# A convolution's products by patches of 4 rows x 2 columns in a four-image convolution, attention and filter kernel

## The chip, the cores and the metric

One Trainium2 chip (trn2), one core. The metric is device time in microseconds. Engines: PE (TensorE matmul), PEld (its weight loads), DVE (VectorE), ACT (ScalarE), POOL (GpSimd), SP (SyncE, which here only issues DMAs). Each engine works through its own queue in order, and waits on semaphores for the others.

## The reference, cut to what matters

Four images of 256 channels, 48 x 48. Layer 0: group norm, 3x3 convolution, scale and shift, ReLU, q, k and v, attention with 8 heads, projection, added to the input. Layer 1: group norm, a 3x3 convolution that gives five sets of nine softmax weights per pixel, five dilated filters with these weights, a 1x1 convolution of the six results, batch norm over all images, added.

```
x = lax.conv_general_dilated(Vx, conv_w, window_strides=(1, 1), padding='SAME', ...)
x = x + conv_b[None, :, None, None]
...
x = jax.nn.relu(x)
...
attn = softmax(einsum('bhdn,bhdm->bhnm', q, k) * scale)
...
guidance = _conv(x, W_cat, pad=1)
for i, d in enumerate((1, 6, 12, 24, 36)):
    w = softmax(guidance[:, 9 * i:9 * (i + 1)], axis=1)
    outs.append(_dyn_branch(x, w, d))
y = _conv(concatenate(outs), W_scale, pad=0)
```

The change touches how the first convolution, `conv_general_dilated`, is computed for images 1 to 3.

## The kernel before

All is float32. Channels lie on 128 partitions in two halves (`NH` = 2). An image passes three stages: the convolution with q, k and v (`conv_qkv`), attention (`attention`), the filters (`dynamic_filters`). Image 0's convolution runs alone. After it, attention of image b alternates with a stage in which the filters of image b run together with the convolution and qkv of image b + 1; the last filters run with two chunks left over from image 2.

The convolution (`conv`) makes four output rows at a time from six input rows. Along rows it uses six sums of input rows, `v[0]` to `v[5]`, each from rows `d[0]` to `d[5]` of the padded, normalized image (`pads[b % 2]`), made in stages by `inputs`: on DVE for image 0, on POOL for the others, with ACT for the multiples by 2 and 4. `ORDER` = (1, 2, 3, 4, 0, 5) is the order of the products. For each of the six there are three weight columns `u[i]`, so a product over 3 columns and two channel halves is six matmuls of 128 x 128 by 288 columns, for each half `g` of the rows and each half `o` of the outputs. `outputs` empties PSUM and combines the six products into four rows; two PSUM banks (tag `c`) take turns. The weights `u` are made once, in image 0 (`Made`), stored in `u_d`, and loaded again by `taken(i)` on SP, 768 KB each, into two buffers.

All code runs through one recording order: each engine's queue follows the order of the Python calls. In the filter stage `drive` decides it. It holds a clock per engine in estimated nanoseconds (`Clock`), and five streams (`loads`, `far`, `near`, `filters`, `mixes`), each of which yields the time from which its next step is due. If none is due by PE's clock, the next step of the filler `other` (convolution, then qkv, of the next image) is issued; a step of it is one or a few matmuls. Before `drive`, at the seam, `run(ns)` issues filler unconditionally: 2400 ns, then 600 and 700 around the parts of `norm.finish`, then 2500 after the normalization.

The seam is this: the last unit of attention is closed (`close`: sums on PE, transposes and reciprocal on DVE), its last chunk is projected (`project`, PE), added to the image and put through `bn_stats` on DVE; `norm.finish` aggregates on DVE, averages over groups on PE, squares on ACT (L665), a second matmul, a square root on ACT (L98), a reciprocal on DVE; then DVE (L636) and ACT (L1661) normalize a half of the image each, and the first matmuls of the filters (`pg`, L1197) can read it. POOL clears `lg`, `bmat` and `amat` (L1179).

In the filter stage, for each of six chunks: `weights` makes softmax weights (`pg`, `pt`, `pw`, `lg`), `far` builds matrices by predicated copies on DVE and multiplies on PE (L1395), copies on ACT or DVE (`moved`, L1170, L1172), `near` multiplies on DVE nine taps (L1461, one operand from PSUM) which POOL adds (L1466), `mixes` does the 1x1 convolution (`py`, L1561). ACT copies each tap's weights into PSUM (`wb`, L1448), one bank of them.

In attention, POOL also issues accumulating DMAs (L1052, L1054) that take over a part of the softmax sums from DVE (L1050).

Of the kernel before, what the change touches and what calls it, by code (L numbers as in the profile page):

```python
# [16 lines left out]
N = HH * WW  # L17
P = 128
# [39 lines left out]
def conv_preact_kernel(  # L58
# [483 lines left out]
    u_d = tc.dram_tile([6, P, NH, 3, C], F32, name="u_d")  # L542
# [3 lines left out]
    with tc.tile_pool(name="w", bufs=1) as wpool, tc.tile_pool(  # L546
        name="act", bufs=1
    ) as act, tc.tile_pool(name="u", bufs=2) as upool, tc.manual_schedule():
# [12 lines left out]
        wqkv = wpool.tile([P, NH, 3, C], F32, tag="wqkv", name="wqkv")  # L561
        wp = wpool.tile([P, NH, C], F32, tag="wp", name="wp")
# [53 lines left out]
        bn_s6 = wpool.tile([P, NH], F32, tag="bn_s6", name="bn_s6")  # L616


        pads = []
        for j in range(2):  # L620
            t = act.tile([P, NH, PADW * PADW], F32, tag=f"pad{j}", name=f"pad{j}")
            t = t.rearrange("p h (r w) -> p h r w", w=PADW)
            nc.gpsimd.memset(t[:, :, 0, :], 0.0)
            nc.gpsimd.memset(t[:, :, PADW - 1, :], 0.0)
            nc.gpsimd.memset(t[:, :, 1 : PADW - 1, 0], 0.0)
            nc.gpsimd.memset(t[:, :, 1 : PADW - 1, PADW - 1], 0.0)
            pads.append(t)

# [58 lines left out]
        class Clock:  # L687
# [11 lines left out]
            def level(self):  # L699
                self.t = dict.fromkeys(self.t, max(self.t.values()))  # L700
# [21 lines left out]
        def taken(i):  # L722

            u = upool.tile([P, NH, 3, C], F32, tag="u", name=f"u_{i}")
            nc.sync.dma_start(out=u, in_=u_d[i])
            return u

        class Made:


            def __init__(self, wc, pool):
                self.w = [wc[:, :, 3 * j : 3 * j + 3, :] for j in range(3)]
                self.u = {}
                self.pool = pool

# [9 lines left out]

            def home(self, i):
                return upool.tile([P, NH, 3, C], F32, tag="u", name=f"u_{i}")
# [4 lines left out]
            def __call__(self, i):  # L752
                w, u = self.w, self.u
                if i in (2, 4):
                    nc.vector.tensor_tensor(u[i], u[i], w[1], ALU.subtract)
                if i == 2:
                    nc.scalar.mul(w[0], w[0], 0.25)
                    nc.scalar.mul(w[1], w[1], 0.5)
                if i in (0, 5):
                    u[i] = self.home(i)  # L760
                    nc.scalar.mul(u[i], w[i and 2], -6.0)
                nc.sync.dma_start(out=u_d[i], in_=u[i])
                return u[i]
# [148 lines left out]

        def conv_qkv(b, gn, psum_tile, weights, ready, pool, between=()):

            hid = keep("h", f"hid_{b}")
            yield from conv(b, gn, psum_tile, weights, ready, pool, hid, between)
# [6 lines left out]
            for c in range(NCK):  # L923
                cols = slice(c * CH, (c + 1) * CH)
                for g in range(NH):
                    for s, dst, bias in ((0, q, Q_B), (1, k_, K_B)):
# [18 lines left out]
                        )  # L945
                        yield 2 * MM
# [31 lines left out]
        def attention(b, q, k_, vT, pools, spare, project, scratch):  # L978
# [132 lines left out]
            weigh(*steps[-1], prev)  # L1111
            close(last)
            return ao, chunk
# [25 lines left out]
        def dynamic_filters(b, ao, chunk, norm, other, pools):  # L1139
# [485 lines left out]
            def drive(streams):  # L1625

                due = [next(s, None) for s in streams]
                while any(d is not None for d in due):
                    soonest = NEVER
                    for j, d in enumerate(due):  # L1630
                        if d is None:
                            continue
                        d = d() if callable(d) else d
                        if d <= clock.t["PE"]:
                            due[j] = next(streams[j], None)
                            break
                        soonest = min(soonest, d)
                    else:
                        got = next(other, None)
                        if got is not None:  # L1640
                            spent[0] += got
                        elif soonest < NEVER:
                            clock.t["PE"] = soonest

            if alone:
                other = late()


            while chunk < NCK:
# [142 lines left out]
        u_next = None  # L1792
        norms = {}
        for b in range(B + 1):

            with tc.tile_pool(name=f"work1_{b}", bufs=2) as work1, tc.tile_pool(
# [13 lines left out]
                if b < B:  # L1810
                    weights, between = taken, ()
                    if b == 0:
# [62 lines left out]
                if b == 0:  # L1875
                    for j, _ in enumerate(other):
                        if j == 0:
# [5 lines left out]
                            nc.vector.tensor_scalar(bn_s6, bn_s, -1.0 / 6.0, None, ALU.mult)  # L1883
                            table(AF.Exp)
# [8 lines left out]
                else:  # L1893
                    if b == B:
# [15 lines left out]
                        for j in range(2):  # L1910
                            t = upool.tile([P, NH, 3, C], F32, tag="u", name=f"yu_{j}")
                            t = t.rearrange("p h k c -> p (h k c)")
                            homes += [unit(t[:, : NH * CH]), unit(t[:, NH * CH :])]
# [48 lines left out]
            scratch = upool.tile([P, NH, 3, C], F32, tag="u", name=f"scratch_{b}")  # L1962
            scratch = scratch.rearrange("p h k c -> p (h k c)")
            spare = []
            if b + 1 < B:
                load_pad(b + 1)
                u_next = taken(ORDER[0])
# [13 lines left out]
            with tc.tile_pool(name=f"work0_{b}", bufs=2) as work0, tc.tile_pool(  # L1981
# [4 lines left out]
                    lambda c, ao, pp, b=b, n=norm1: project(b, c, ao, pp, n), scratch,  # L1986
# [76 lines left out]
```

## Time and profile before

| | |
|---|---|
| median of 3 runs | 2771.2 us (2770.79 to 2772.4) |
| the profiled execution's own time | 2766.55 us |
| its span | 2764.8 us |
| granted TensorE clock, mean | 0.99 |
| HBM read and written | 107.40 MB, 34.46 MB |
| image 0's convolution and qkv | 0 to 148 us |
| attention 0 | 148 to 515 us |
| filters 0 with convolution 1, to its last `py` | to 747 us |
| rest of convolution 1, and its qkv | to 817 us |

The stages of images 1 and 2 follow in the same manner, and the last filters with the batch norm end the kernel. A line of the page's list of groups, or of a timeline, gives: start and length (timeline), engine, source line, operation, written tile <- read tiles, partitions x elements, count, and in brackets the engine's idle time before it with what ended it. One float32 matmul of the program appears as two records of PE. A clock of 0.5 in a window is half rate.

### The profile page before, as it was taken

The numbers are of one execution on the slowest core, as the hardware profiler recorded it, in microseconds if no ns is written. First come the engines' busy times: TensorE is split into PE (matmuls) and PEld (weight loads), VectorE is DVE, ScalarE is ACT, GpSimd is POOL, SyncE is SP. The second block draws the span as 40 slices with busy tenths as digits, with TensorE's granted clock in tenths as the row PEclk, the third lists the DMA queues.
The fourth block names the chain that finished last, engine by engine and source line by source line (L and its number), as shares of the span: only waits on it lengthen the run. The fifth ranks groups of instructions, "written<-read, shape, count | busy, mean of one in ns | idle before, by whom it ended". The sixth has DMA issues, their size and how long they took to land. (4 is left out here: it accounts for less than half of the span.)

```text
span 2764.8 us, 42248 instructions
## 1 busy us (share of the span) xinstructions
PE 2638.8 (95%) x17108; PEld 1135.8 (41%) x17108; DVE 2025.3 (73%) x1956; ACT 1761.1 (64%) x2153; POOL 632.3 (23%) x583
## 2 busy tenths in 40 slices
PE   7999999899999999989999999999999999999994
PEld 5632223455662222345565222245566222234452
DVE  6578888656539888856644988894664988885476
ACT  3488988633349888843336889882335988873244
POOL 5100100435400100054430001006542001000352
PEclk9999999999999999999999999999999999999997
DMA  5604544223422444423360345442335244432465
GB/s 216 156 24 103 109 98 104 58 77 90 104 56 58 101 102 97 109 57 75 84 132 9 81 98 112 101 87 56 93 92 150 55 96 95 101 87 68 118 181 182
DMA packets 132522, 267.35 MB, mean 97 GB/s; under 512 B 55656, under 2 KB 97552, under 8 KB 131424
## 3 DMA queue, kind: packets, MB, share of 16 engines
q0 software_dynamic: 25952, 135.74, 21.6%
q1 hardware_dynamic: 106368, 128.84, 17.7%
q8 instruction: 136, 2.23, 0.3%
q14 instruction: 66, 0.54, 0.1%
HBM read 107.40 MB, written 34.46 MB: 51 GB/s over the span
## 5 line engine op out<-in xcount | busy, mean ns | idle before, releaser
L1050 DVE TENSOR_TENSOR acc<-acc,p 128x2048 f32<-128x2048 f32 (+1 forms) x572 | 1061.1, 1855 | 115.6 <-ACT p L1014 64.9
L1014 ACT ACTIVATE p<-se 128x1536 f32<-128x1536 f32 x648 | 938.7, 1449 | 0.1
L1005 PE MATMUL so<-q,k 32*128 32x512 f32 (+1 forms) x1440 | 726.4, 592 | 13.5 <-ACT p L1013 12.7
L1005 PE MATMUL se<-q,k 32*128 32x512 f32 (+1 forms) x4320 | 735.1, 592 | 0.0
L1034 PE MATMUL num<-p,vT 128*32 128x512 f32 (+1 forms) x5760 | 705.1, 560 | 4.6 <-ACT p L1014 2.4
L1013 ACT ACTIVATE p<-so 128x512 f32<-128x512 f32 x648 | 388.4, 599 | 186.8 <-PE se L1005 80.0
L1466 POOL TENSOR_TENSOR near<-near,prod 128x768 f32<-128x768 f32 x192 | 348.8, 1817 | 431.4 <-DVE prod L1461 424.7
L1005 PEld LDWEIGHTS so<-q,k 32*128 32x128 f32 x1440 | 216.1, 183 | 529.0 <-ACT p L1013 489.8
L1034 PEld LDWEIGHTS num<-p,vT 128*32 128x32 f32 x5760 | 133.8, 108 | 478.8 <-issue 444.3
L1054 POOL DMA_DIRECT2D scratch<-p x124 | 105.5, 851 | 772.3 <-ACT p L1014 519.8
L1461 DVE TENSOR_TENSOR prod<-wb,pad 128x768 f32<-128x768 f32 x192 | 181.9, 953 | 87.6 <-ACT wb L1448 75.6
L1561 PE MATMUL py<-far,wsc 128*128 128x384 f32 x704 | 236.7, 488 | 0.0
L1005 PEld LDWEIGHTS se<-q,k 32*128 32x128 f32 x4320 | 226.7, 183 | 5.4 <-ACT p L1014 4.1
L1448 ACT COPY wb<-ws 128x384 f32<-128x384 f32 x216 | 108.7, 507 | 171.3 <-DVE prod L1461 137.6
L1170 ACT COPY far<-far 128x512 f32<-128x512 f32 x82 | 87.9, 1099 | 137.4 <-PE far L1395 134.6
L1052 POOL DMA_DIRECT2D scratch<-p x32 | 17.9, 559 | 669.7 <-ACT p L1014 508.3
L1561 PEld LDWEIGHTS py<-far,wsc 128*128 128x128 f32 x704 | 131.1, 190 | 87.3 <-issue 1.8
L897 PE MATMUL pc<-cv_q,u 128*128 128x288 f32 x576 | 151.8, 415 | 8.2 <-DVE cv_q L788 6.2
L1197 PE MATMUL pg<-pad,wcat 128*45 128x384 f32 x864 | 149.1, 493 | 10.0 <-ACT lg L1255 4.4
L897 PE MATMUL pc<-cv_k,u 128*128 128x288 f32 x576 | 153.3, 410 | 4.3 <-DVE yt L832 2.7
L930 PE MATMUL pq<-hid,wqkv 128*128 128x384 f32 x384 | 125.6, 487 | 1.7 <-DVE yt L832 0.6
L897 PEld LDWEIGHTS pc<-cv_q,u 128*128 128x128 f32 x576 | 108.7, 192 | 43.2 <-DVE cv_q L788 6.3
(252 smaller groups left out, 2368.3 us busy)
## 6 DMA issues: line engine op xcount, KB each, us to landing
scratch<-p POOLq DMA_DIRECT2D x156, 768.0 KB, 5.7
ws<-w_d SPq DMA_DIRECT2D x216, 192.0 KB
pad<-in_x SPq DMA_DIRECT2D x14, 1152.0 KB
u<-u_d SPq DMA_DIRECT2D x18, 768.0 KB
xst<-in_x POOLq DMA_DIRECT2D x36, 192.0 KB, 6.9
x_d<-pad SPq DMA_DIRECT2D x36, 192.0 KB
y_d<-y SPq DMA_DIRECT2D x14, 384.0 KB
u_d<-u SPq DMA_DIRECT2D x6, 768.0 KB
```

What stands on the lines that cost most here:

```text
L897: nc.tensor.matmul(m, u[:, h, kx, o * P : (o + 1) * P], halves[g][:, h, i, :, kx : kx + WW], start=(h == 0 and kx == 0), stop=(h == NH - 1 ...
L930: nc.tensor.matmul(pq[:, :CH], wqkv[:, i, s, g * P : (g + 1) * P], hid[:, i, cols], start=(i == 0), stop=(i == NH - 1),)
L1005: nc.tensor.matmul(dst[:, at : at + n], k_[r, g, m * P : (m + 1) * P], q[r, g, q0 : q0 + n], start=True, stop=True,)
L1013: nc.scalar.activation(p[:, 0, :], s1, AF.Exp, scale=QS)
L1014: nc.scalar.activation(p[:, 1:, :], s3, AF.Exp, scale=QS)
L1034: nc.tensor.matmul(st["num"][r, at : at + n], vT[:, m, g * P + j * D : g * P + (j + 1) * D], p[:, j, at : at + n], start=(m == 0 and not s ...
L1050: nc.vector.tensor_tensor(st["acc"][:, js], other[:, js], p[:, js], ALU.add)
L1197: nc.tensor.matmul(pg[64 * s : 64 * s + NG, :CH], wcat[:, ii, k, :], shifted(ii, cc, k // 3 - 1, k % 3 - 1), start=(i == 0 and k == 0), st ...
L1448: nc.scalar.copy(pw[:, :CH], fetched[c, k][0])
L1461: nc.vector.tensor_tensor(prod.rearrange("p h (r w) -> p h r w", w=WW), wb, src, ALU.mult)
L1466: nc.gpsimd.tensor_tensor(cat, cat, prod, ALU.add)
L1561: nc.tensor.matmul(py[c][:, o, :CH], wsc[:, n * NH + i, o * P : (o + 1) * P], rhs, start=(n == 0 and i == 0), stop=(n == order[-1] and i = ...
```

## The change

Image 0 keeps its convolution. Images 1 to 3 get `conv_blocks`. The rows are handled as before, but the columns too: each `v[i]` is combined along columns, at stride 2, into four operands (`along`), and four products (weights `f0` to `f3`, made from the three columns of `u[i]`) give two output columns. A tile is one product i and one output half o, both row halves together: 12 tiles of four column products of two matmuls each, 128 x 128 by 288 columns. The four are combined into `y` by `one`, `two` and further adds.

- `Made.convert` makes the four weight columns in image 0 with two ACT multiplies and three DVE adds per output half, in `pads[1]`, and stores them; `taken(t)` loads a tile's 512 KB into one of three places of `ring`, two tiles ahead.
- The sums of rows (`stage0` to `stage3`) are POOL instructions of 1200 elements, with multiples on ACT. `stage0` is issued by `following[0]()`, ahead of `close(last)` in attention. The column sums of the first three products are on POOL, the others where `either` finds the earlier clock, POOL or DVE.
- PSUM is emptied by ACT, or by DVE where the planner's `busy_dve` is false.
- `drive` asks `need[0]` before it issues filler: if the next step's operand or bank isn't there by the planner's clock, the filler yields and the clock moves on. `level` no longer pulls POOL's clock to the others', and at the seam it is set to PE's plus 12,500 ns.
- Sums, products and results live in the tiles of k, q and v and, for the operands of products 4, 0 and 5, in the pad, so `clear` zeroes its border again at the start of each attention.

```diff
+            def convert(self):
+
+                i = self.ready.pop()
+                four = pads[1].rearrange("p h r w -> p (h r w)")
...
+                for o in range(NH):
...
+                    nc.scalar.mul(f[:, :, 0], of[:, :, 0], 2.0)
+                    nc.scalar.mul(f[:, :, 3], of[:, :, 2], 2.0)
+                    tt = nc.vector.tensor_tensor
+                    tt(f[:, :, 1], of[:, :, 0], of[:, :, 2], ALU.add)
+                    tt(f[:, :, 2], f[:, :, 1], of[:, :, 1], ALU.subtract)
+                    tt(f[:, :, 1], f[:, :, 1], of[:, :, 1], ALU.add)
+                    nc.sync.dma_start(out=u_d[i, o], in_=t)
...
+            def sum(self, out, x, y, op):
+                nc.gpsimd.tensor_tensor(out, x, y, op)
+                return clock("POOL", 2800)
+
+            def stage0(self):
+
+                v, d = self.v, self.d
+                nc.scalar.mul(v[0], d[2], 4.0)
+                nc.scalar.mul(v[5], d[1], 4.0)
+                self.sum(v[0], d[4], v[0], ALU.subtract)
+                self.sum(v[5], d[3], v[5], ALU.subtract)
+                self.sum(v[1], v[0], v[5], ALU.add)
+                self.along(1)
+                self.sum(v[2], v[0], v[5], ALU.subtract)
+
+            def stage1(self):
+
+                v, d = self.v, self.d
+                nc.scalar.mul(v[6], d[3], 2.0)
+                nc.scalar.mul(v[4], d[1], 2.0)
+                clock("ACT", 2600)
+                self.sum(v[3], d[4], d[2], ALU.subtract)
+                self.sum(v[6], v[6], v[4], ALU.subtract)
+                self.sum(v[4], v[3], v[6], ALU.subtract)
+                self.sum(v[3], v[3], v[6], ALU.add)
+
+            def stage2(self):
+
+                v, d = self.v, self.d
+                self.sum(v[0], v[0], d[2], ALU.subtract)
+                nc.scalar.mul(v[6], d[0], 4.0)
+                self.sum(v[5], d[5], v[5], ALU.subtract)
+                self.sum(v[0], v[0], v[6], ALU.add)
+                clock("ACT", 1300)
+
+            def stage3(self):
+
+                v, d = self.v, self.d
+                nc.scalar.mul(v[6], d[3], 4.0)
+                clock("ACT", 1300)
+                self.sum(v[5], v[5], v[6], ALU.subtract)
...
+        def either(out, a, c, op, *after):
+
+            part = 0.5 if len(out.shape) == 2 and out.shape[-1] == XN else 1.0
+            if clock.t["POOL"] + 1400 * part <= clock.t["DVE"] + 1000 * part:
+                nc.gpsimd.tensor_tensor(out, a, c, op)
+                return clock("POOL", 1400 * part, *after)
+            nc.vector.tensor_tensor(out, a, c, op)
+            return clock("DVE", 1000 * part, *after)
...
+        def conv_blocks(b, psum_tile, blocks, pool, hid):
...
+            blocks.stage1()
+            need[0] = lambda: 150 + max(slot("c", 2), blocks.end[STEPS[0]])
+            for t, (i, o) in enumerate(TILES):
+                u = us.pop(t)
...
+                for n, j in enumerate((1, 2, 0, 3)):
+                    m = psum_tile(f"pc_{b}_{i}_{o}_{j}")[:, :XN]
+                    clock("PE", 0, slot("c", 2), blocks.end[i, j])
...
+                    for h in range(NH):
+                        nc.tensor.matmul(
+                            m, u[:, h, j], z[:, h], start=(h == 0), stop=(h == NH - 1)
+                        )
+                        clock("PE", MM * XN / CH)
+                        if h == 0:
+                            need[0] = lambda: 0.0
+                            if n == 0:
+                                if t + 2 < len(TILES):
+                                    us[t + 2] = taken(t + 2)
+                                if (i, o) == (ORDER[0], 0):
+                                    blocks.along(ORDER[1])
+                                elif (i, o) == (ORDER[0], 1):
+                                    blocks.along(ORDER[2])
+                                    blocks.stage2()
+                                elif (i, o) == (ORDER[1], 1):
+                                    blocks.stage3()
+                                before(i, o)
+                            yield MM * XN / CH
+                    if n == 0:
+                        one = pool.tile([P, XN], F32, tag="one", name=f"one_{b}_{i}_{o}")
+                        nc.scalar.copy(one, m)
...
+                    elif n == 1:
...
+                        if busy_dve():
+                            nc.scalar.copy(two[:, 1], m)
...
+                            either(two[:, 0], one, two[:, 1], ALU.add, end)
+                            either(two[:, 1], one, two[:, 1], ALU.subtract, end)
+                        else:
+                            tt(two[:, 0], m, one, ALU.add)
+                            tt(two[:, 1], one, m, ALU.subtract)
...
             weigh(*steps[-1], prev)
+            following[0]()
             close(last)
+            following[1]()
...
-                        got = next(other, None)
-                        if got is not None:
-                            spent[0] += got
-                        elif soonest < NEVER:
-                            clock.t["PE"] = soonest
+                        open_at = need[0]()
+                        if open_at <= clock.t["PE"]:
+                            got = next(other, None)
...
+                        soonest = min(soonest, open_at)
+                        if soonest < NEVER:
+                            clock.t["PE"] = max(soonest, clock.t["PE"])
...
+            clock.level()
+            if not alone:
+                clock.t["POOL"] = clock.t["PE"] + 12500
...
+                def opened(b=b):
+                    coming.append(Blocks(b + 1, pads[(b + 1) % 2]))
+                    coming[-1].stage0()
+                    us[1] = taken(1)
+
+                following = [opened, lambda: None]
```

## The prediction

> **What bounds the kernel now.** I read first the busy shares, then the busy time by stage, and then the timeline of one seam between two stages, engine by engine.
>
> ```profile
> PE 2638.8 (95%) x17108; PEld 1135.8 (41%) x17108; DVE 2025.3 (73%) x1956; ACT 1761.1 (64%) x2153; POOL 632.3 (23%) x583
> ```
>
> ```profile
> 515.00:530.00 15.00, 10.28 (x47) 4.98 (x48) 8.06 (x12) 6.36 (x11) 7.56 (x8) 0.77 0.05 12
> 530.00:747.00 217.00, 211.79 (x976) 124.16 (x975) 126.73 (x173) 73.56 (x125) 115.75 (x68) 1.00 0.31 78
> 747.00:771.00 24.00, 24.00 (x100) 18.67 (x99) 10.63 (x26) 8.64 (x15) 0.00 (x0) 1.00 0.93 191
> 771.00:817.40 46.40, 46.40 (x170) 31.91 (x168) 14.21 (x28) 19.24 (x33) 0.12 (x1) 1.00 0.19 43
> ```
>
> The columns after the length are the busy time of PE, PEld, DVE, ACT and POOL, the granted clock, DMA share and GB/s. The rows are the end of attention 0, the filters of image 0 with the convolution of image 1 as filler, the rest of that convolution alone, and its qkv. PE is full in the last two and 98% full in the first long one: what PE is spared there is spared by the kernel, as long as the other engines keep up. The same pattern follows twice more, after attention 1 and 2.
>
> The seam itself, from the timelines of ACT, DVE, POOL and PE:
>
> ```profile
> 513.68 1.45 ACT L1014 ACTIVATE p<-se 128x1536 f32<-128x1536 f32 x1
> ...
> 533.37 0.20 ACT L98 ACTIVATE gstd_n<-gstd_n 128x2 f32<-128x2 f32 x1 [0.94 <-DVE gstd_n L97]
> ...
> 534.99 2.30 ACT L1661 ACTIVATE pad<-pad,gshift_n,grstd_n 128x2304 f32<-128x2304 f32 x1
> ```
>
> ```profile
> 516.12 2.29 DVE L1050 TENSOR_TENSOR acc<-acc,p 128x2048 f32<-128x2048 f32 x1
> ```
>
> ```profile
> 522.36 0.42 POOL L1179 MEMSET lg<- 128x384 f32 x1 [18.31 <-DVE ao L1087]
> ...
> 523.71 1.35 POOL L786 TENSOR_TENSOR cv_q<-pad,cv_q 128x600 f32<-128x600 f32 x1
> 525.02 1.34 POOL L787 TENSOR_TENSOR cv_q<-pad,cv_q 128x600 f32<-128x600 f32 x1
> 526.44 1.45 POOL L788 TENSOR_TENSOR cv_q<-cv_q 128x600 f32<-128x600 f32 x1
> 527.84 1.46 POOL L789 TENSOR_TENSOR cv_q<-cv_q 128x600 f32<-128x600 f32 x1
> ...
> 536.23 2.60 POOL L794 TENSOR_TENSOR cv_q<-pad 128x600 f32<-128x600 f32 x1
> ```
>
> ```profile
> 522.28 5.23 PE L1120 MATMUL pp<-ao,wp 128*128 128x384 f32 x8 [2.75 <-DVE ao L1087]
> ...
> 537.54 2.16 PE L1197 MATMUL pg<-pad,wcat 128*45 128x384 f32 x12 [1.39 <-DVE pad L636]
> ```
>
> See here that the filters start (L1197 at 537.54) when the second norm is ready, that this goes through ACT's square root L98 at 533.37, and that nothing stands before L98 on ACT.
>
> **Removed: PE work.** A matmul of 288 columns shows as two records; twelve of them end 5.82 us after the twelve before (next fence), so one costs 0.485 us. An image falls from 6 x 2 x 2 x 6 = 144 to 12 x 4 x 2 = 96. Three images: 144 x 0.485 = **-69.8 us**.
>
> ```profile
> 65.47 5.98 PE L897 MATMUL pc<-cv_k,u 128*128 128x288 f32 x24
> 71.30 5.98 PE L897 MATMUL pc<-cv_q,u 128*128 128x288 f32 x24
> ```
>
> All of it lies on the path. In the instruction order of the changed kernel nothing of the convolutions of images 1 and 2 comes after the last `py`: the filters' stretch holds 96 conv and 16 qkv matmuls (57.0 us) where 90 conv matmuls stood (43.7), and behind it stay 36.5 us instead of 73.1. +13.3 - 36.6 = -23.3 per image, the same sum.
>
> **Added: a wait at the head of ACT.** In that order `following[0]()` puts `stage0` ahead of `close(last)`. The generator starts `stage1` at its first call, and its ninth yield, inside `run(700)`, issues `stage2`, so ACT's multiply `v[6] = 4 d[0]` stands between the squares of `norm.finish` and its square root. It overwrites the `v[6]` that the last sum of `stage1` reads, and its wait names that POOL sum. The walk: ACT's two multiplies follow the exponential that ends at 515.13; the first takes twice a half's 0.6, to 516.4. POOL is free but DVE's `acc` add of two SBUF operands runs from 516.12 to 518.41, and I let POOL wait for it. A 1200-element sum is two halves: 2 x 1.31 with one operand from `pad` (523.71 to 525.02), 2 x 1.41 otherwise; a 576-element product 1.40. So v0, v5 5.24; v1 2.82; four products 5.6; v2 2.82; the memsets 1.35 (522.36 to 523.71); `stage1` 2.9 + 3 x 2.82 = 11.4: 29.2 us, until 547.6. With the multiply's 1.3 the square root comes at 548.9, not 533.37: 15.5 us late. Behind it on ACT are the table load, the normalization of half 1 and the copy `one` of the second tile; DVE's reciprocal and normalization wait for it, PE's third product of that tile waits for `one`, its fourth for DVE's pair (0.9) behind that, and `pg` stands behind them: another 1.6. PE has 15 conv matmuls ahead of `pg`, as before, and no others. **+17.1 per image.** Bounds: 14.4 if POOL isn't held and a sum costs 2.74 (from 1.45 at 600 and 1.81 at 768 elements); 19.8 if products cost as the 1.81 of L1466 and a second hold like L794's 1.1 comes. I stay at 17.1, built from the same shapes' halves.
>
> PE then idles some 18 us. In the trace idle gaps of 1.4 and 2.75 us around 520 are followed by a slow `pp`: 5.23 us, against 2.85 for the same eight records in the middle of attention 1. The start of the kernel shows it after a long idle: 24 records in 8.91 us, not 5.98.
>
> ```profile
> 19.65 8.91 PE L897 MATMUL pc<-cv_q,u 128*128 128x288 f32 x24 [6.22 <-DVE cv_q L788]
> ```
>
> So **+2.6** (2.4 to 2.9) each time. The Trainium skill ("TensorE: Matmul & The Clock Gate", What's actually happening) gives half rate until one busy window of about 3.4 us has passed; by that an estimate is 1.7, and the sum 2.7 us less in all.
>
> **Added: DVE, ACT and POOL work under the filters.** Counted over the changed order, a filters' stretch gets on DVE 27 adds of 288 (0.457) and 26 of 576 (about 0.75, from 0.78 at 600) with both operands in SBUF, and 11 that read PSUM (0.45): 37 us. ACT gets some 10 us more than before, POOL some 32; their cover is the 217 us stretch with ACT at 74 and POOL at 116. But two-SBUF adds meet POOL:
>
> ```profile
> L856 DVE TENSOR_TENSOR cs<-cs x16: 457/457/1951, 73.2 to 2072.8; 128x288 f32<-128x288 f32 x16
> ```
>
> The two long ones fell into `near` adds; adds that read PSUM keep their 0.45 there. Before, the convolution's two-SBUF adds ran after the filters except in the third image. I counted three stretches, each from the first `far` product of chunk 1, 2 or 4 to that of the next: PE 29.8 / 40.9 / 28.3, DVE 23.2 / 28.8 / 21.9 with 8 / 13 / 9 such adds, POOL 21.8 / 23.0 / 17.3. Nothing is lost if the adds find POOL idle. If each waits the full 1.49 seen, DVE has 73.9 + 30 x 1.49 = 118.6 against PE's 99.0: 20 us. POOL runs 63% of that time; at 0.63 x 1.1 DVE has 95 of 99 us, full but not over. ACT's `wb` copies wait for DVE's `prod`, and ACT's copies that empty PSUM stand behind them; a bank now holds 0.97 us of work, not 2.9. I take **+7** per image, near a third of the upper bound.
>
> The Trainium skill ("GPSIMD Engine Reference", Engine selection) advises VectorE for elementwise adds, as about 2x slower on GPSIMD. The trace has 1.45 us against 0.78 for 600 elements, 1.86x; at 2x the walk's sums grow by some 7%, 2 us per image.
>
> **Added: weights in image 0.** 36 DVE adds of 256 elements at some 0.42 and 24 ACT multiplies at 0.4 lie under a PE-bound stage (DVE 88.7, ACT 57.7 busy of its 148 us): **+1**, 0 to 5 if the six blocks of 2.5 us keep PSUM copies waiting beyond a bank's 2.9. Nothing for the loads: 12 of 512 KB per image for 6 of 768 KB on SP's queue, issued two tiles (7.8 us of PE) ahead; a late one would cost its transfer, 2.4 us at the 216 GB/s of the first slice. What stands behind one on SP (`ws`, `w_d`) was issued behind such a wait before too. The `clear` memsets run on POOL in attention, where it is busy 31 of 367 us.
>
> **Sum.** -69.8 + 3 x (17.1 + 2.6 + 7) + 1 = +11.3. The profiled execution took 2766.55, 4.65 below the median of 2771.2: 2777.9 there, **2782.5** as a median.
>
> **Rivals.** (a) The stall and the crowding stay at their low ends or below: the square root is late by 8 to 14, DVE's adds mostly find POOL idle. For it: POOL can start its sums 5 us earlier than before, and the planner sets POOL's clock 12.5 us ahead. Against: the wait is fixed in ACT's order. -69.8 + 3 x (14.4 + 2.4 + 3) = -10 gives 2761; with 8 us and 1 us, 2740. (b) The terms cancel: opening 16, crowding 5: -69.8 + 70.8 + 1, 2773. (c) DVE becomes the bound: the adds wait the full length of POOL's, 20 us per image; it decides from a mean wait of 0.84 us, where DVE's 73.9 reaches PE's 99.0 (25.1 / 30). -69.8 + 3 x 39.7 + 1 = +50, 2821. (d) The filler doesn't fit and PE idles away what it was spared, up to 2842; the order speaks against it.
>
> **How the numbers follow.** Forecast 2782.5, chance 0.40, own range 2777 to 2797; (a) 0.27; (b) 0.16; (c) 0.15; (d) 0.02. The range 2750 to 2815 leaves out the far ends of (a), (c) and (d). About 0.2%, 5.5 us, can be told from no change: faster 0.27, same 0.16, slower 0.57.
>
> **What would show it.** Right: L98's square root near 549 with ACT idle before the 1200-element multiply, released by POOL; PE idle for 15 us or more before `pg` at all three seams, the clock down after it; filters' to qkv's end 23 us shorter in PE's work; two-SBUF adds on DVE well above 0.457 and 0.75. Wrong: POOL's `stage1` over by 540, or PE under 90% busy in the filters' stretch after `pg` (then (c)).

## The result, and the profile after

The changed kernel takes 2816.4 us (median of 4 runs, 2812.73 to 2820.33) against 2771.8 for the kernel before beside it: a ratio of 1.0161, 95% interval 1.0143 to 1.0178. It is slower, and 1.4 us above the range of the prediction. Its profiled execution has a span of 2815.0 us, 50.2 more than before.

First the busy shares of the changed kernel:

```profile
PE 2607.1 (93%) x16820; PEld 1093.7 (39%) x16820; DVE 2129.0 (76%) x2041; ACT 1800.3 (64%) x2251; POOL 740.7 (26%) x644
```

PE is 31.7 us less busy and not 70, though the instructions are gone; DVE has 104 us more and POOL 108. Then busy time by stage, of the first seam, of the filters of image 0 and of what comes after them (columns as in the prediction: length, then PE, PEld, DVE, ACT, POOL, then the granted clock):

```profile
519.60:560.60 41.00, 19.30 (x94) 10.29 (x93) 16.76 (x26) 14.88 (x19) 37.59 (x22) 0.78 0.17 48
560.60:801.20 240.60, 225.90 (x982) 128.82 (x982) 164.55 (x208) 90.86 (x165) 121.57 (x74) 0.97 0.27 74
801.20:837.40 36.20, 36.20 (x139) 25.86 (x137) 10.36 (x21) 14.83 (x26) 0.12 (x1) 1.00 0.81 156
```

The same three stages of before, cut at the same instructions:

```profile
513.20:537.50 24.30, 17.82 (x92) 10.14 (x92) 14.18 (x19) 13.31 (x22) 14.98 (x13) 0.86 0.18 50
537.50:744.70 207.20, 203.34 (x937) 117.77 (x938) 121.35 (x165) 67.55 (x115) 108.33 (x63) 1.00 0.31 76
744.70:817.40 72.70, 72.70 (x278) 52.34 (x277) 25.87 (x55) 28.74 (x50) 0.12 (x1) 1.00 0.44 93
```

The seam is 16.7 us longer, with PE idle for more than half of it. The filters are 33.4 us longer, and the rest 36.5 shorter. In the filters' stretch PE is busy for 225.9 us where the same work at full clock would take 218: the granted clock is 0.97, and was 1.00.

All stages, in us. "Idle" is the stage's length less PE's busy time; "cold" is half of PE's busy time inside the records in which the granted clock is 0.5.

| stage | before | after | change, images 1, 2, 3 |
|---|---|---|---|
| image 0, to the first attention | 147.9 | 154.4 | +6.5 |
| seams, attention's end to `pg` | 24.3, 23.7, 24.4 | 41.0, 41.0, 40.5 | +16.7, +17.3, +16.1 |
| filters and what follows, to the next attention | 279.9, 280.1, 253.6 | 276.8, 275.4, 249.2 | -3.1, -4.7, -4.4 |
| in it, idle | 3.9, 4.0, 7.8 | 14.7, 14.1, 17.6 | +10.8, +10.1, +9.8 |
| in it, cold | 0, 0, 0 | 8.0, 7.1, 7.9 | +8.0, +7.1, +7.9 |
| four attentions, sum | 1468.0 | 1473.1 | +5.1 |

So 6.5 + 50.1 - 12.2 + 5.1 = 49.5 of the 50.2 us, and the rest is in the last filters.

**The seam** is the walk of the prediction. Timelines of ACT, POOL and PE of the changed kernel:

```profile
538.20 0.48 ACT L670 ACTIVATE gd_n<-mvn,gmean_n 128x1 f32<-128x1 f32 x2
552.04 1.20 ACT L1009 ACTIVATE cv_v<-pad 128x1200 f32<-128x1200 f32 x1 [13.37 <-POOL cv_k L980]
553.15 0.19 ACT L98 ACTIVATE gstd_n<-gstd_n 128x2 f32<-128x2 f32 x1
```

```profile
549.30 2.71 POOL L980 TENSOR_TENSOR cv_k<-cv_k,cv_v 128x1200 f32<-128x1200 f32 x1
```

```profile
557.39 3.25 PE L1130 MATMUL pc<-cv_v,ring 128*128 128x288 f32 x6 [16.44 <-ACT one L1150]
560.57 2.80 PE L1481 MATMUL pg<-pad,wcat 128*45 128x384 f32 x8
```

ACT has the squares done at 538.7 and stands for 13.37 us before a multiply that waits for POOL's last sum of `stage1`, which ends at 552.0. The square root comes behind the multiply, the copy `one` behind the root and the normalization, and PE's next product, after 16.44 us, behind the copy. It then runs at half rate, 3.25 us for six records that took 1.62 before:

```profile
534.53 1.62 PE L897 MATMUL pc<-cv_k,u 128*128 128x288 f32 x6
```

**The filters' stretch** lost in small waits. PE's waits there (total, times, longest, in us):

```profile
PE xa L1599 <- DVE own L1456: 5.2, 3, 2.8
PE pq L1211 <- ACT hid L1078: 3.1, 1, 3.1
PE pw L1535 <- DVE e L1531: 2.9, 2, 1.9
```

DVE is busy for 68% of the stretch (164.55 of 240.60 us), but it is nearly full in the 10 us before the waits of 2.76 and of 1.75 us for `own`:

```profile
664.57:674.57 10.00, 7.24 (x36) 4.65 (x35) 9.57 (x10) 7.72 (x13) 6.18 (x4) 1.00 0.26 84
733.74:743.74 10.00, 7.05 (x36) 4.45 (x34) 9.22 (x11) 8.58 (x14) 3.97 (x3) 1.00 0.23 41
```

What one of the waits costs beyond itself is seen in PE's timeline and in a window right behind it:

```profile
674.57 0.63 PE L1599 MATMUL xa<-ident,own 128*128 128x128 f32 x4 [2.76 <-DVE own L1456]
...
677.29 5.49 PE L1845 MATMUL py<-near,wsc 128*128 128x384 f32 x8 [0.52 <-POOL near L1750]
```

```profile
676.00:682.90 6.90, 6.38 (x22) 3.35 (x24) 5.23 (x7) 0.13 (x2) 3.10 (x2) 0.51 0.13 51
```

In a stretch in which PE is otherwise nearly full, the clock falls to half 1.4 us after a wait of 2.76 us and stays there for 6.8. Eight records of 384 columns take 5.49 us; at full rate they take 2.85. With half of the window's 6.38 us of PE's time, the wait costs 6 us in all.

**Image 0.** PE's third group of products waits 4.12 us for ACT's copy `m` and then runs cold (before: 1.41 and 6.09 us). ACT's timeline shows multiplies of the first conversion right before the batch norm's square root, with the copies `m` behind both. The root itself waits for `bn_s_f` of DVE, where six adds of the conversion (26.92 to 29.50) stand ahead. Changed kernel, then before:

```profile
32.27 8.76 PE L935 MATMUL pc<-cv_k,ring 128*128 128x288 f32 x24 [4.12 <-ACT m L881]
```

```profile
29.34 0.40 ACT L773 ACTIVATE pad<-ring 128x256 f32<-128x256 f32 x1
30.21 0.20 ACT L98 ACTIVATE bn_s_f<-bn_s_f 128x2 f32<-128x2 f32 x1 [0.47 <-DVE bn_s_f L97]
```

```profile
29.98 6.09 PE L897 MATMUL pc<-cv_k,u 128*128 128x288 f32 x24 [1.41 <-ACT m L843]
27.93 0.19 ACT L98 ACTIVATE bn_s_f<-bn_s_f 128x2 f32<-128x2 f32 x1
```

### The profile page after: what moved, and what is told of

Its sections match the earlier page's. It is cut to its first block, busy times and chain, and to the rows that moved or that the text cites. A ratio compares the mean times of both kernels' runs of the same rounds, so it can differ in the third digit from the quotient of the medians.

```text
span 2815.0 us, 42056 instructions
## 1 busy us (share of the span) xinstructions
PE 2607.1 (93%) x16820; PEld 1093.7 (39%) x16820; DVE 2129.0 (76%) x2041; ACT 1800.3 (64%) x2251; POOL 740.7 (26%) x644
## 5 line engine op out<-in xcount | busy, mean ns | idle before, releaser
L1287 PE MATMUL so<-q,k 32*128 32x512 f32 (+1 forms) x1440 | 727.1, 592 | 17.4 <-ACT p L1295 16.7
L1336 POOL DMA_DIRECT2D ring<-p x124 | 105.5, 851 | 774.0 <-ACT p L1296 438.1
L1334 POOL DMA_DIRECT2D ring<-p x32 | 17.9, 558 | 630.4 <-ACT p L1296 458.9
L1454 ACT COPY far<-far 128x512 f32<-128x512 f32 x93 | 98.1, 1105 | 120.1 <-PE far L1679 118.0
L1481 PE MATMUL pg<-pad,wcat 128*45 128x384 f32 x864 | 157.9, 517 | 3.1 <-ACT lg L1539 1.9
L1211 PE MATMUL pq<-hid,wqkv 128*128 128x384 f32 x384 | 131.6, 499 | 12.5 <-ACT hid L1078 11.0
L1332 DVE TENSOR_TENSOR acc<-p,p 128x2048 f32<-128x2048 f32 x36 | 82.3, 2285 | 23.5 <-ACT p L1296 23.5
L1211 PEld LDWEIGHTS pq<-hid,wqkv 128*128 128x128 f32 x384 | 73.2, 193 | 65.7 <-ACT hid L1078 12.8
L1456 DVE COPY far<-far 128x512 f32<-128x512 f32 x51 | 55.4, 1087 | 52.2 <-PE far L1679 51.5
```

What stands on the lines that cost most here:

```text
L1211: nc.tensor.matmul(pq[:, :CH], wqkv[:, i, s, g * P : (g + 1) * P], hid[:, i, cols], start=(i == 0), stop=(i == NH - 1),)
L1287: nc.tensor.matmul(dst[:, at : at + n], k_[r, g, m * P : (m + 1) * P], q[r, g, q0 : q0 + n], start=True, stop=True,)
L1332: nc.vector.tensor_tensor(st["acc"][:, js], other[:, js], p[:, js], ALU.add)
L1336: nc.gpsimd.dma_start(out=extra, in_=p[:, 1:], accum_op=ALU.add)
L1481: nc.tensor.matmul(pg[64 * s : 64 * s + NG, :CH], wcat[:, ii, k, :], shifted(ii, cc, k // 3 - 1, k % 3 - 1), start=(i == 0 and k == 0), st ...
```

## The experiments

Stage times of every kernel, in us (image 0 is the start of attention 0; the filters are counted to the next attention's start; idle and cold are those of the first filters and their rest). Executions of the same code differ by up to 3 us in image 0 (154.4 and 157.3 in after and e10) and in a seam (27.4 and 24.4 in e11). The ratio is against the kernel before, timed beside it.

| kernel | image 0 | seams | filters and rest | idle, cold | median | ratio (95%) |
|---|---|---|---|---|---|---|
| before | 147.9 | 24.3, 23.7, 24.4 | 279.9, 280.1, 253.6 | 3.9, 0 | 2771.8 | |
| after | 154.4 | 41.0, 41.0, 40.5 | 276.8, 275.4, 249.2 | 14.7, 8.0 | 2816.4 | 1.0161 (1.0143 to 1.0178) |
| e1 | 154.7 | 26.0, 27.3, 27.2 | 279.0, 279.6, 250.5 | 16.7, 7.7 | 2781.4 | 1.0048 (1.0031 to 1.0065) |
| e2 | 157.1 | 41.1, 40.7, 40.5 | 274.8, 275.0, 248.5 | 14.2, 6.5 | 2818.5 | 1.0176 (1.0159 to 1.0193) |
| e3 | 155.2 | 41.0, 41.0, 40.5 | 272.2, 271.8, 253.9 | 14.2, 3.5 | 2810.7 | 1.0146 (1.0129 to 1.0163) |
| e4 | 154.6 | 41.0, 40.7, 40.0 | 277.1, 278.7, 248.5 | 13.7, 8.3 | 2842.3 | 1.0259 (1.0242 to 1.0276) |
| e5 | 152.2 | 24.7, 24.5, 30.2 | 277.5, 277.4, 250.5 | 16.9, 7.4 | 2788.2 | 1.0063 (1.0045 to 1.0082) |
| e6 | 149.5 | 24.7, 23.7, 24.3 | 275.2, 274.9, 263.7 | 17.3, 3.7 | 2784.8 | 1.0070 (1.0048 to 1.0091) |
| e7 | 150.8 | 25.9, 26.7, 25.4 | 294.4, 292.4, 264.3 | 31.5, 9.6 | 2827.9 | 1.0209 (1.0192 to 1.0226) |
| e8 | 149.5 | 24.6, 28.5, 26.9 | 272.0, 270.8, 242.0 | 12.9, 4.9 | 2754.2 | 0.9953 (0.9936 to 0.9970) |
| e9 | 154.5 | 41.0, 40.9, 40.5 | 264.7, 264.3, 238.9 | 9.1, 1.7 | 2786.8 | 1.0066 (1.0048 to 1.0085) |
| e10 | 157.3 | 41.1, 41.0, 40.5 | 264.5, 264.2, 239.2 | 9.0, 1.7 | 2786.8 | 1.0064 (1.0047 to 1.0081) |
| e11 | 149.4 | 27.4, 24.4, 24.2 | 275.0, 276.6, 249.4 | 14.7, 6.7 | 2765.8 | 0.9994 (0.9981 to 1.0007) |
| e12 | 154.8 | 41.0, 40.7, 40.5 | 266.3, 263.5, 237.8 | 8.5, 4.1 | 2783.8 | 1.0042 (1.0026 to 1.0059) |

**e1: the seam alone.**

```diff
                                     blocks.along(ORDER[2])
+                                elif (i, o) == (ORDER[1], 0):
                                     blocks.stage2()
```

> The call of stage2 moves from the second tile of a blocks convolution to its third, so ACT's multiply 4 d[0] comes after the copies of the first two filters' pg and no longer between the squares and the square root of the second norm. Theory (the seam's extra 16.7 us is this multiply waiting for POOL's stage1): from attention's end to pg takes 24 us again, not 41, at all three seams, the filters' stretches stay near 240, and the median falls by 50 to 58 us, to 2758 to 2766. Rival (POOL is late whatever stands on ACT, and the third tile, which needs POOL's next products at about 562, gives it back): the seam falls too, but the filters' stretches grow by 10 us or more each, and the median stays at 2790 to 2816.

The seams fell by 15.0, 13.7 and 13.3 us, the median by 35. The mechanism is the theory's. Two things fell short of it. The filters gave back 2.2, 4.2 and 1.3 us, a small part of the rival. And 2 to 3 us of the seam stayed, which ACT's timeline of e1 explains:

```profile
541.09 0.20 ACT L98 ACTIVATE gstd_n<-gstd_n 128x2 f32<-128x2 f32 x1 [0.94 <-DVE gstd_n L97]
...
542.72 2.30 ACT L1955 ACTIVATE pad<-pad,gshift_n,grstd_n 128x2304 f32<-128x2304 f32 x1
544.92 0.37 ACT L1151 COPY one<-pc 128x288 f32<-128x288 f32 x1
```

The root no longer waits for POOL, but `one` of the second tile still stands behind the root, a table load and the normalization of 2.30 us, and PE waits 2.93 us for it.

**e2: the first conversion later.** The call in image 0 leaves out `ORDER[1]`, and the next one makes two.

```diff
-                if self.ready:
+                while self.ready and i != ORDER[1]:
                     self.convert()
-                self.ready = [i]
+                self.ready.append(i)
```

> In image 0 the first conversion is left until weights(3) is called, where two are made in a row; the others keep their places. Theory (image 0 lost its 6.5 us at the first block, which stands ahead of the batch norm's square root and of the copies that empty the first two banks): PE's wait before the third product group is 1.4 us again, not 4.12, its 24 records take 6 us, not 8.76, attention 0 starts 5 us earlier (near 149), and the median is about 2811. Rival (all six blocks cost about 1 us each by holding up ACT's copies): attention 0 starts within 2 us of 154.4 and the median stays at 2814 to 2817.

Neither came. PE's wait at the third group fell to 2.68 us, but a new one of 3.71 us appeared, for DVE's pairs `cs`, which now stood behind 5 us of conversion, and the group behind it took 7.57 us. Attention 0 started no earlier. The loss goes with a block of conversion in front of whatever empties a bank, so the repair has to cut the block. That was tried from e5 on, together with the rest of the seam:

```diff
+                        if o == 0 and at and len(weights.ready) > NH:
+                            weights.convert()
                         yield MM * TN / CH
...
-                run((600, 700)[at])
+                run((600, 1000)[at])
```

Here `convert` makes one output half and stands behind the copies of a bank, one product later than before; and one matmul more goes ahead of the second norm's root, so that `one` is copied before it. e11 has e1's edit and these two, and nothing else:

> The changed kernel with the repairs of image 0 (conversion in halves behind the copies) and of the seam (stage2 in the third tile, the second tile's copy one before the square root) and nothing else. Theory (the three losses add up independently): 2816.4 less 5 to 7 for image 0 and less 3 times 15 to 17.5 for the seams: 2757 to 2766, faster than before by 0.2% or more. Rival (a seam gives back in the filters, as e1's stretches grew by 3 us): 2768 to 2776, the same as before.

2765.8 us is the upper edge of the theory's range, and against before it is the same within the interval. Image 0 is at 149.4 and the seams at 24.2 to 27.4. PE's third group in e11:

```profile
30.36 6.09 PE L933 MATMUL pc<-cv_k,ring 128*128 128x288 f32 x24 [1.79 <-ACT m L879]
```

The wait is 1.79 us and the 24 records are as quick as before the change. e5 to e8 have the same edit of image 0, with 149.5 to 152.2 us. With both repairs, what the kernel still loses lies in the filters.

**e3, e4, e7: other engines for the work in the filters.** e3 lets DVE empty PSUM itself and gives every choice of `either` to POOL; e7 gives it to POOL too, with ACT emptying PSUM; e4 puts the copies of `own` on ACT.

```diff
-                return clock.t["DVE"] > max(clock.t["ACT"], clock.t["PE"]) + 500
+                return False
...
-            if clock.t["POOL"] + 1400 * part <= clock.t["DVE"] + 1000 * part:
+            if True:
```

> Every sum or product that chose between POOL and DVE goes to POOL, and the pairs and results are always made by DVE straight from PSUM (before, ACT copied the bank whenever DVE was behind by the planner's clock, and an add of two SBUF operands followed). DVE keeps no add of two SBUF operands in the blocks convolution but the multiply-adds. Theory (the filters' excess of 20 us over PE's added work is DVE's adds waiting for POOL, which makes DVE late for PE and drops the clock): DVE's time over the shortest of each shape falls from 23.9 to under 12 us per stretch, the stretch from 240 to about 225 to 230, the median to 2771 to 2790. Rival (it is lateness in the order of the engines, wherever the adds stand: POOL's products of 1.4 to 1.8 us make the results late instead): stretches of 238 to 248, median 2810 to 2840.

> Both copies of own go to ACT, instead of to the engine that is free first by the planner's clock. Theory (PE's longest wait in the filters' stretch, 5.2 us in 3 waits for own on DVE, and the clock that drops after each, are worth 7 to 9 us per stretch): the waits of xa for own fall under 1.5 us, the stretch from 240 to 232, the median to about 2790 to 2796. Rival (lateness goes round: another wait, for two, hid or the filters' e, takes its place): the stretch stays within 3 us of 240, the median at 2808 to 2822.

> Image 0 and the seams as in e5_slack. Filters: ACT copies every bank out of PSUM, POOL makes every add and product, and DVE keeps of the blocks convolution only the multiply-adds. Theory (DVE's adds crowd DVE and meet POOL; e3 took them from DVE too but let DVE empty PSUM behind its filters' work, 8 us of waits for that): waits for own, e and two all fall under 2 us, idle under 8 and cold under 3, the stretch near 228; rival (POOL, then busy some 175 of 235 us, makes near and the results late): waits for near and hid of 8 us or more, the stretch over 238. Median 2750 to 2765, or 2780 to 2800.

In its first two stretches with their rest e3 has the theory's sign and a third of its size (-4.6 and -3.6 us), in the last the rival's (+4.7). DVE's time over the shortest of each shape fell from 23.9 to 10.9 us and cold time from 8.0 to 3.5, but idle time stayed at 14, with a new first wait:

```profile
PE pc L1130 <- DVE two L1161: 8.0, 4, 3.2
```

Its 217 us for the stretch alone are no gain: less filler found a place there, and 55 us of it follow, not 36. In e4 the waits for `own` fell to 1.8 us and those for `hid` and for a bank took their place: the rival. (Its total is worse for another reason: the last image's filters, which the edit touches too, took 12 us longer, and its attention 8.) In e7 POOL is busy for 194.6 of 269.8 us, and PE waits for it and for what comes behind it:

```profile
PE pq L1213 <- ACT hid L1078: 10.0, 2, 7.0
PE pc L1130 <- POOL pad L1055: 8.6, 2, 5.1
```

**e5, e6: the planner.** e5 meets every due time 1 us later, e6 counts 1.5 us for DVE's adds of 576 elements.

> Three edits in three stages, read stage by stage. Image 0: each conversion is made in two halves behind the copies that empty a bank, one tile later. Theory: no block stands before the batch norm's square root any more and none of 5 us before the pairs, attention 0 starts at 148 to 150; rival: ACT's multiplies wait for DMA out of the same buffer and hold up copies, it starts after 153. Seams (stage2 in the third tile, and one matmul more before the square root, so that the second tile's copy one stands before it): theory, 24 to 25 us instead of e1's 26 to 27; rival, the added matmul costs what it saves. Filters: every due time of the images 0 to 2, of the filters' steps and of the filler, is met 1 us later by the planner's clock, so that PE's order holds more filler before each step. Theory (PE waits because the planner takes DVE's results for done up to 3 us too early): idle and cold time of a stretch, 14.7 and 8.0 us, fall by half, the stretch to 230; rival (lateness adds up whatever the margin): the stretch stays at 238 to 245. Median 2755 to 2765 if all three theories hold, 2775 to 2785 if the filters' one fails.

> Image 0 and the seams as in e5_slack. Filters: the planner counts 1.5 us, not 1.0, for an add of 576 elements that either gives to DVE (half of that for 288). Theory (the order is wrong only by what contention adds to these adds, 24 us per stretch): the waits of xa for own and of pw for e fall from 8 to 10 us to under 4, the stretch from 240 to 230 or less; rival (DVE's order, not its planned time, decides): within 4 us of 240. Median 2755 to 2765, or 2772 to 2785.

Image 0 and the seams followed the theory (e5's 152.2 and its third seam apart), the filters the rivals. In e5 PE's order did change: its first stretch holds 1040 records of PE, for 982 in the changed kernel. The waits for `own` on DVE fell from 5.2 to 1.4 us, but others grew or came, and idle time rose from 14.7 to 16.9:

```profile
PE pw L1537 <- DVE e L1533: 4.3, 2, 2.5
PE pc L1130 <- DVE cv_k L1172: 4.1, 1, 4.1
```

e6 lost the waits for `own` and half of the cold time, but idle time rose to 17 and, with more work on POOL, the filters of image 2 outlasted their filler by 23 us.

**e9, e10, e12: work cut.** In these the planner counts as before and PE's order is that of the changed kernel. e9 makes DVE's adds of `either` on an eighth of their columns and leaves out the rest, e10 POOL's too, e12 POOL's alone and with them the additions to `near` (for images 0 to 2). A result that would read the first half of a pair `two` reads the second in all three. e9's edit, and e12's of `near`:

```diff
-            nc.vector.tensor_tensor(out, a, c, op)
+            n = out.shape[-1] // 8
+            nc.vector.tensor_tensor(out[..., :n], a[..., :n], c[..., :n], op)
...
-                    nc.gpsimd.tensor_tensor(cat, cat, prod, ALU.add)
+                    n = CH if alone else CH // 8
+                    nc.gpsimd.tensor_tensor(cat[:, :, :n], cat[:, :, :n], prod[:, :, :n], ALU.add)
```

> The changed kernel, but every sum or product of the blocks convolution that either gives to DVE works on an eighth of its columns; the rest of the output of these sums is left out. The planner's clock, and so PE's order, are as in the changed kernel. Theory (what the filters' stretch has lost, 10.8 us of idle and 8 of cold clock, comes from DVE being filled with these adds and made to wait for POOL by them): the waits for own and e fall under 1 us, idle to 4 to 7, cold under 2.5, the stretch from 240 to 225 to 229, the median to 2775 to 2790. Rival (POOL's and ACT's part or PE's order itself): the stretch stays above 234, the median above 2800.

> As e9_dve_eighth, and POOL's sums and products that either gave it are cut to an eighth too. Theory (DVE alone is the cause): within 3 us of e9_dve_eighth per stretch. Rival (POOL's share counts as much, by meeting DVE's remaining work and by near): 4 us or more below e9_dve_eighth per stretch, 12 or more in the median.

> The changed kernel, but in the stretches of images 0 to 2 POOL's additions to near, and the sums and products that either gives it, work on an eighth of their columns; the rest of these sums is left out. DVE keeps all its adds, 47 in a stretch with 27 us of work at their shortest and 19 us of waiting; the planner's clock, and so PE's order, are as in the changed kernel. It tells the two halves of e9_dve_eighth's 12 us apart. Theory (the waiting for POOL counts: it is what makes single results 2 to 3 us late, and the clock falls only after such waits): DVE's time over the shortest falls from 23.9 to under 8 us, cold from 8.0 to under 3, idle from 14.7 to under 10.5, the stretch from 240 to 228 to 231, the median to 2778 to 2792. Rival (the 27 us of added work alone fill DVE's order, whoever meets POOL): the stretch stays at 235 to 240, the median at 2800 to 2816.

Busy time in the first filters' stretch of e9 and of e12:

```profile
563.80:792.40 228.60, 219.46 (x982) 126.74 (x982) 142.63 (x208) 90.50 (x166) 119.05 (x74) 0.99 0.28 77
```

```profile
562.80:792.90 230.10, 221.63 (x982) 127.70 (x982) 144.90 (x208) 90.47 (x165) 41.87 (x74) 0.98 0.30 77
```

With what follows, both are 10 to 12 us shorter than the changed kernel in each of the three stretches, and e10 adds nothing to e9. Idle time fell less than expected of e9 (9.1 for 4 to 7), cold time as expected, to 1.7; e12 came as its theory had it, but for cold time (4.1 for under 3). The same adds of DVE in the changed kernel and in e12 (shortest, median and longest in ns, then first and last start):

```profile
L1057 DVE TENSOR_TENSOR two<-one,two x13: 447/452/1961, 590.0 to 740.9; 128x288 f32<-128x288 f32 x13
L1057 DVE TENSOR_TENSOR cv_v<-cv_k,cv_v x2: 758/1502/2246, 595.1 to 643.3; 128x576 f32<-128x576 f32 x2
```

```profile
L1058 DVE TENSOR_TENSOR two<-one,two x13: 446/450/533, 591.6 to 735.0; 128x288 f32<-128x288 f32 x13
L1058 DVE TENSOR_TENSOR cv_v<-cv_k,cv_v x2: 758/792/825, 596.8 to 643.5; 128x576 f32<-128x576 f32 x2
```

In e12 the adds have their full work, and no long one is left but one of 2.99 us beside a sum of `stage3` that was not cut. Over the shortest of their shape, the 47 adds of the stretch lose 19.6 us in the changed kernel, 3.9 in e12 and 11.4 in e9. So the added 27 us of work alone are not what the stretch pays for: e12 keeps them, drops 15.7 us of waiting for POOL, and gains what e9 gains. That the waiting alone counts is not shown either: e9 drops 17 us of the work and only 8 of the waiting. What the two share is less time on DVE, 142.63 and 144.90 us for 164.55. e12 also brings POOL's own results sooner (41.87 us busy for 121.57), which no run takes apart from the rest; e10, with POOL's part of `either` cut beside DVE's, gains nothing over e9.

DVE's adds of 288 elements that read PSUM do not wait: in e3's first stretch, 37 of them, 29 at a time when POOL was busy, took 0.44 to 0.46 us. That agrees with the Trainium skill ("SBUF — State Buffer", Who interferes with whom): a DVE instruction with two SBUF inputs contends with a GpSimd instruction that reads SBUF, one with at most one SBUF input, outside the 2-port perf modes, does not.

What remains in the first stretch of e9 and e12 against before is 4.6 to 5.2 us of idle time and 1.7 to 4.1 of cold. Its waits are of 2.1 us or less, for `hid`, `e`, `own`, `two` and `one`. They look like the steps' own latencies, now that a bank holds 0.97 us of products and not 2.9; that was not tried by itself.

**e8: the order, only where PE waits.** e11 with three later places in PE's order:

```diff
-                    yield lambda: max(slot("k", banks_k) + 150, at + 150)
+                    yield lambda: max(slot("k", banks_k) + 150, at + 2150)
...
-                yield clock("DVE", 1100 if pair else 320) + 150
+                yield clock("DVE", 1100 if pair else 320) + 2150
...
                         relus(NEVER)
+                        done = clock.t["ACT"] + 3000
+                        need[0] = lambda: max(150 + slot("c", 2), done)
```

> Image 0 and the seams as in e6_costs. In the filters the planner keeps its costs, but three steps for which PE was seen waiting are put into PE's order later: the transposes of own 2 us later, those behind e 2 us later, and the first qkv product of the filler 3 us behind the last relu (e5_slack moved all steps and the filler alike, which changed their order little). Theory (PE waits because just these results come later than planned): waits for own, e and hid fall from 11 to 13 us to under 4 per stretch, idle and cold time from 23 to about 12, the stretch with its tail from 277 to about 266, the median to 2740 to 2755. Rival (another late result takes their place, as in e4_own_act and e5_slack): stretch with tail 274 to 280, median 2765 to 2785.

2754.2 us, 0.9953 of before (0.9936 to 0.9970): faster than both kernels. The filters with their rest are 3.0, 5.8 and 7.4 us shorter than e11's, and the waits for `own`, `e` and `hid` fell from 11.3 to 1.7 us. New waits of 7.5 us came:

```profile
PE pc L1130 <- ACT one L1151: 4.1, 2, 2.6
PE pc L1130 <- ACT cv_k L1167: 3.4, 3, 2.3
```

So part of the rival holds too, and the median is at the upper end of the theory's range. The three places were moved together, so that no run says what each is worth.

## Why the prediction was right or wrong

Its direction was right, and its cause at the seams. It was 33.9 us short of the median (2816.4 for 2782.5).

- **PE's work.** Right. Idle and cold time left out, filters and rest fell from 276.0 to 254.1, 276.1 to 254.1 and 245.8 to 223.7 us, 22 each for the 23.3 forecast; the parts behind the last `py` became 36.5, 36.5 and 35.5 shorter, for 36.6.
- **The wait at the head of ACT.** Right in place and cause, and nearly in size: +16.7, +17.3 and +16.1 for 17.1. That the sizes are so close is in part luck. The root came 31.6 us after the last exponential's end at 521.5, where the walk had 33.8, so it was 13.4 us late and not 15.5; the way from there to `pg` grew by 3.3 us and not 1.6, and 1.6 of that is the cold clock, which the sum held as a term of its own. e1 took the multiply away and with it 13 to 15 us.
- **Cold clock at the seam.** It is there, but 1.6 us of it lie inside the seam's 41 (3.25 for 1.62 in the last product), and about 1.4 behind `pg`; the 2.6 was in part counted twice.
- **Crowding, "+7 per image, near a third of the upper bound".** This is the step that failed. Filters and rest changed by -3.1, -4.7 and -4.4, against -23.3 of work: 20.2, 18.6 and 18.9 us lost, where 7 + 2.6 stood in the sum. It accounts for 29 of the 39 us that the profiled sum (+11.3 for +50.2) missed. The size of the waiting was in the bounds: 0.42 us for each of 47 adds (19.6 over 47) beside the 1.49 of the upper end. What went wrong was the price: I let the loss begin where DVE's busy sum reaches PE's over three spans of 28 to 41 us, at a mean wait of 0.84 us. DVE is busy 68% of the stretch, and PE lost nevertheless: DVE is nearly full for 10 us at a time (92 and 96% before the waits for `own`). PE's order is fixed, so that one result 2 to 3 us late stops it for as long, whatever DVE has to spare later; and in this kernel the stops of 1.92 us and of 2.76 to 3.11 us were all followed by half rate for 3.4 or 6.8 us, for which the term had nothing. e12 and e9 put 10 to 12 us of the loss on the time that DVE's adds take, work and waiting together; the rest, 7 to 10, is left open above.
- **Rival (c)**, at 2821, is the nearest number, but not for its reason: it needed DVE as the bound of the whole stretch. Its sign to look for, PE under 90% busy behind `pg`, did not show either (225.9 of 240.6, 94%, and still 91% without the 8.0 us of cold time, which count as busy).
- **Weights in image 0, "+1, 0 to 5".** +6.5. I bounded it by a bank's 2.9 us of cover for blocks in the middle of the stage; the first block stands at its start, ahead of the batch norm's root and of the first copies, and brought a cold clock too. In the five kernels with the conversion in halves image 0 takes 1.5 to 4.3 us more than before.
- **Attention**, 5 us in all, was not foreseen. In image 3 it was 6.8, with PE idle for 4.0 of the first 46.6 us and the clock at 0.96; in e3, whose filters of image 2 ended earlier in the stage, that attention took 366.6 us as before. The cause was not tried.

## What to carry to other kernels

Where one engine's order is fixed ahead and full, price a busier helper by how late its single results become, each with the clock's fall behind it, and not by whether its busy sum still fits a whole stage. Before an instruction is put into another engine's queue, ask what its operands wait for and what is queued behind it: here one multiply of 1.2 us cost 42 us in three places, and taking it out of the way changed no arithmetic and gave the median 35 of them back. A planner that counts an add's shortest time for an add that meets POOL was mended where its lateness stopped PE (e8); a margin on every step (e5) only moved the waits to other results.

## What the runs showed of the hardware

- The granted clock fell after waits much shorter than I had thought of. In the changed kernel's stretches, waits of 1.92 us and of 2.76 to 3.11 us were all followed by half rate, for 3.4 or 6.8 us, and those of 1.76 were not. Length alone does not decide: in e9 waits of 1.75 were, in two cases of three, in e3 all three of 1.46 were, and both of 3.21 were not. (Those of 1.92, 1.75 and 1.46 us, all for `e`, have one of 0.62 close behind them.) The Trainium skill ("TensorE: Matmul & The Clock Gate", What's actually happening) names at least one idle window of about 3.4 us for that. The half-rate records of these stretches are 3.4 or 6.8 us long, but waits of 2.76 us, with PE at work on both sides, were enough.
- Cutting an add's columns to an eighth does not shorten its wait for POOL:

```profile
L1058 DVE TENSOR_TENSOR two<-one,two x13: 183/196/2060, 591.7 to 735.0; 128x36 f32<-128x36 f32 x13
```

An add of 36 columns in e9 takes 0.18 us alone and 2.06 beside a sum of POOL.
